# Moving layer 0's transposed state in rows of 128 bytes, so that the stationary tiles of the mix are contiguous

## Chip, cores, metric

One core of a Trainium2 chip. The metric is the time of one execution on the device in microseconds; the median of several runs is quoted. Everything is fp32.

## The reference, cut to what matters

64 graphs of 256 nodes and 128 features go through four layers. Layer 0 is a gated graph network of five steps; each step multiplies the state h by the adjacency (the mix), then updates it by gates. Layers 1 to 3 do not touch the change.

```python
def step(h, _):                                    # h: (graph, node, feature)
    m_in = jnp.einsum('nm,bmd->bnd', in_matrix, h) # the mix; in_matrix = out_matrix = adj
    ...
    z = jax.nn.sigmoid(av @ w3_w.T + w3_b + u3)
    r = jax.nn.sigmoid(av @ w4_w.T + w4_b + u3)
    hv = jnp.tanh(av @ w5_w.T + w5_b + (r * h @ u5_w.T + u5_b))
    h = (1.0 - z) * h + z * hv
```

## The kernel before

Graphs are handled in 32 pairs. A list scheduler puts the operations of all pairs in order ahead of time, from costs written in the code, so the order on TensorE is fixed and some pairs are always in flight together. The gates work on hT (features on the partitions, 4 chunks of 128 nodes along the row). The mix needs the nodes on the partitions, so after every step but the last, hT is turned into htok: VectorE transposes blocks of 32x32 into S, and four moves, one for each group of 32 source partitions, spread S over the 128 partitions of htok. Partition 4s+x then holds node 32x+s of each chunk, and aTs is the adjacency with its rows in that order.

```python
def turn(src, dst):
    S = flat("S", 3)
    add(DVE, 690, lambda: nc.vector.transpose(S.ap.rearrange("p (x r c) -> p x c r", x=4, c=4),
                                              src.ap.rearrange("p (c x s) -> p x c s", x=4, c=4)), [src], [S], [S])
    def f():
        for k in range(4):
            nc.sync.dma_start(dst.ap[:, 32 * k:32 * k + 32].rearrange("p r c -> p (r c)"),
                              S.ap[32 * k:32 * k + 32].rearrange("s (x f) -> s x f", x=4))
    add(SP, 1720, f, [S], [dst], [dst])

def mix(src, m, also, chunk=lambda src, c: src.ap[:, c, :]):
    t = bank()
    def f():
        for b in range(2):
            for j in range(2):
                nc.tensor.matmul(t.ap[:, b * N:(b + 1) * N], chunk(src, 2 * b + j), m.ap[:, j, :],
                                 start=(j == 0), stop=(j == 1))
    ...
# in the step loop: s = 0 reads x, the four others read htok
    copy(ACT, mT, mix(h, aTs, [mT], lambda src, c: src.ap[:, :, c]) if s else mix(h, aT, [mT]))
    ...
    h = temp([P, D, 4], "htok", 4)
    turn(hT, h)
```

htok is stored [feature][chunk]: a packet of a move is 32 features x 4 chunks x 4 B = 512 contiguous bytes, but the stationary tile of a chunk is 128 words at a step of 4 words.

## Time and profile before

| | before |
|---|---|
| time, median of 3 runs | 1771.41 us (1770.87 to 1772.53) |
| TensorE busy | 1692.9 us, 96% |
| matmuls with htok as stationary tile | 1024 instructions: two for each of 4 matmuls in 128 mixes |
| weight load of an htok tile / of a tile of the same shape from x | 325 / 198 ns |
| block transpose on VectorE | 1120 ns, 128 times |
| moves into htok | 512, of 64 KB, in packets of 512 B |

TensorE is pipelined: an htok matmul lasts 404 ns in the record, and the next one starts 233 ns after it. What counts is the spacing from one start to the next. Weight loads (PEld) overlap the matmuls, and in the record each other too (325 ns long, 233 ns apart); a load is called hidden here as long as it does not lengthen the spacing. The prediction shows the lines and how they are read.

### The profile page before, as it was taken

Reading aid. Unit: us, or ns where it says so; the run is one execution under the profiler, and the core shown is the slowest. Engines: PE = TensorE matmul, PEld = TensorE weight load, DVE = VectorE, ACT = ScalarE, POOL = GpSimd, SP = SyncE. Lnnn points to the kernel's source line nnn. Section 1 sums busy time; section 2 is a strip of 40 time slices with the busy share of each in tenths; the row PEclk is TensorE's granted clock in tenths of the full one; section 3 lists DMA queues with packets and bytes.
Section 4 is the critical chain, followed back from the end, with each engine's and each line's share of the span. In section 5 each row is a group of like instructions: output and inputs, shape, how many; then the busy total and the mean of one; then the engine's idle time right before and its main releaser. Section 6 shows DMA issues by size and latency. Waiting matters only on the chain.

```text
span 1771.8 us, 22424 instructions
## 1 busy us (share of the span) xinstructions
PE 1692.9 (96%) x7408; PEld 1231.7 (70%) x7408; DVE 1315.7 (74%) x3581; ACT 785.6 (44%) x1573; POOL 459.4 (26%) x487
## 2 busy tenths in 40 slices
PE   8999999999999999999999999999999999988764
PEld 5667777777777677776767777777777776755553
DVE  6577867877786887778678878878867788776543
ACT  3445444444453544445444454554444444443221
POOL 0023222222222232213323313233221223322122
PEclk9999999999999999999999999999999999998866
DMA  4100111111111111110111111101111111000000
GB/s 121 39 19 19 43 30 31 30 31 37 30 31 31 40 27 30 31 35 21 38 33 28 27 37 31 30 25 37 30 31 32 29 28 34 19 19 18 18 1 12
DMA packets 109042, 54.35 MB, mean 31 GB/s; under 512 B 9472, under 2 KB 108544, under 8 KB 108928
## 3 DMA queue, kind: packets, MB, share of 16 engines
q1 hardware_dynamic: 108640, 52.40, 11.7%
q8 instruction: 59, 0.97, 0.2%
q10 hardware_dynamic: 288, 0.53, 0.1%
q14 instruction: 55, 0.45, 0.1%
HBM read 10.95 MB, written 8.39 MB: 11 GB/s over the span
## 4 chain that ended last, share of the span: by engine, by line
PE 88%; DVE 6%; ACT 2%; POOL 1%; issue 1%; DMA 1%; SPq 1%; POOLq 0%; DVEq 0%; ACTq 0%
PE ps L459 25%; PE ps L538 7%; PE ps L535 7%; PE ps L551 7%; PE ps L553 7%; PE ps L543 7%; PE ps L687 6%; PE ps L471 6%; PE ps L434 5%; PE ps L646 3%; PE ps L696 3%; PE ps L593 2%; PE ps L635 2%; DVE st L488 1%; DVE o L517 1%
## 5 line engine op out<-in xcount | busy, mean ns | idle before, releaser
L498 POOL TENSOR_SCALAR rs<-mv 128x4 f32<-128x4 f32 x160 | 60.8, 380 | 985.4 <-DVE mv L490 976.5
L459 PEld LDWEIGHTS ps<-aTs,htok 128*128 128x128 f32 x1024 | 254.2, 325 | 40.6 <-issue 18.8
L459 PE MATMUL ps<-aTs,htok 128*128 128x256 f32 x1024 | 265.3, 404 | 10.8 <-DMA htok<-S 10.0
L499 POOL TENSOR_TENSOR rs<-rs,neg_half 128x4 f32<-128x4 f32 x192 | 212.8, 1109 | 194.6 <-DVE rs L492 178.2
L478 ACT COPY mT<-ps 128x512 f32<-128x512 f32 x160 | 93.6, 586 | 228.0 <-PE ps L459 227.8
L557 DVE TENSOR_TENSOR hv<-hv,hT 128x512 f32<-128x512 f32 x160 | 117.5, 738 | 76.5 <-ACT hv L555 75.9
L546 ACT ACTIVATE tz<-ps,bz 128x512 f32<-128x512 f32 x160 | 109.9, 688 | 139.3 <-PE ps L543 138.7
L548 DVE SCALAR_TENSOR_TENSOR tr<-tr,hT 128x512 f32<-128x512 f32 x160 | 118.2, 740 | 68.1 <-ACT tr L541 67.5
L541 ACT ACTIVATE tr<-ps,br 128x512 f32<-128x512 f32 x160 | 109.6, 687 | 130.5 <-PE ps L538 130.0
L555 ACT ACTIVATE hv<-ps,bh 128x512 f32<-128x512 f32 x160 | 109.8, 687 | 125.5 <-PE ps L553 125.1
L538 PE MATMUL ps<-mT,w4s 128*128 128x512 f32 x320 | 164.0, 598 | 1.4 <-ACT mT L478 1.4
L553 PE MATMUL ps<-tr,u5h 128*128 128x512 f32 x320 | 163.4, 596 | 1.5 <-DVE tr L548 1.4
L551 PE MATMUL ps<-mT,w5s 128*128 128x512 f32 x320 | 164.0, 595 | 0.0
L535 PE MATMUL ps<-hT,W 128*128 128x512 f32 x320 | 162.4, 596 | 1.0 <-DVE hT L560 1.0
L543 PE MATMUL ps<-mT,dw 128*128 128x512 f32 x320 | 162.4, 594 | 0.0
L442 DVE STREAM_TRANSPOSE S<-hT 128x512 f32<-128x512 f32 x128 | 142.3, 1120 | 1.8 <-issue 0.4
L459 PE MATMUL ps<-aT,x 128*128 128x256 f32 x512 | 126.4, 391 | 0.0
L511 ACT ACTIVATE x<-y,nmr,rs 128x128 f32<-128x128 f32 x256 | 105.1, 484 | 30.6 <-DVE nmr L506 30.5
L560 DVE SCALAR_TENSOR_TENSOR hT<-hv,hT 128x512 f32<-128x512 f32 x160 | 115.8, 727 | 1.8
L558 DVE SCALAR_TENSOR_TENSOR hv<-tz,hv 128x512 f32<-128x512 f32 x160 | 115.4, 724 | 1.4
L434 PEld LDWEIGHTS ps<-ident,x 128*128 128x128 f32 x512 | 65.3, 144 | 71.8 <-issue 26.2
L459 PEld LDWEIGHTS ps<-aT,x 128*128 128x128 f32 x512 | 98.5, 199 | 21.4 <-issue 7.2
(160 smaller groups left out, 2975.1 us busy)
## 6 DMA issues: line engine op xcount, KB each, us to landing
htok<-S SPq DMA_DIRECT2D x512, 64.0 KB, 2.1
x<-x_in SPq DMA_DIRECT2D x32, 256.0 KB, 2.9
y_out<-o SPq DMA_DIRECT2D x32, 256.0 KB, 2.3
W<-mats_in SPq DMA_DIRECT2D x1, 832.0 KB, 6.2
W<-mats_in ACTq DMA_DIRECT2D x1, 512.0 KB, 4.1
rbc<-rows_in SPq DMA_DIRECT2D x1, 385.0 KB, 6.9
aT<-adjT_in SPq DMA_DIRECT2D x1, 256.0 KB, 5.2
aTs<-adjT_in SPq DMA_DIRECT2D x2, 128.0 KB, 4.8
```

The costliest lines, as they stand in the source:

```text
L434: nc.tensor.transpose(t.ap[:, c * P:(c + 1) * P], chunk(c), ident.ap)
L442: add(DVE, 690, lambda: nc.vector.transpose(S.ap.rearrange("p (x r c) -> p x c r", x=4, c=4), src.ap.rearrange("p (c x s) -> p x c s", x=4 ...
L459: nc.tensor.matmul(t.ap[:, b * N:(b + 1) * N], chunk(src, 2 * b + j), m.ap[:, j, :], start=(j == 0), stop=(j == 1))
L499: nc.gpsimd.tensor_tensor(rs.ap, rs.ap, neg_half.ap, op=ALU.pow)
L535: add(PE, 865, lambda tg=tg: nc.tensor.matmul(tg.ap, mat("u3"), hT.ap, start=True, stop=False, skip_group_check=True), [hT, W0], [tg], [tg ...
L538: add(PE, 865, lambda tg=tg, mT=mT: nc.tensor.matmul(tg.ap, w4s.ap, mT.ap, start=False, stop=False, skip_group_check=True), [mT, w4s], [tg])
L543: add(PE, 865, lambda tg=tg, mT=mT: nc.tensor.matmul(tg.ap, dw.ap, mT.ap, start=False, stop=True, skip_group_check=True), [mT, dw], [tg])
L548: add(DVE, 690, lambda tr=tr: nc.vector.scalar_tensor_tensor(tr.ap, tr.ap, 1.0, hT.ap, op0=ALU.add, op1=ALU.mult), [hT], [tr])
L551: add(PE, 865, lambda tv=tv, mT=mT: nc.tensor.matmul(tv.ap, w5s.ap, mT.ap, start=True, stop=False), [mT, w5s], [tv], [tv, hv])
L553: add(PE, 865, lambda tv=tv, tr=tr: nc.tensor.matmul(tv.ap, u5h.ap, tr.ap, start=False, stop=True), [tr, u5h], [tv])
L557: add(DVE, 690, lambda hv=hv: nc.vector.tensor_sub(hv.ap, hv.ap, hT.ap), [hT], [hv])
L560: add(DVE, 690, lambda hv=hv: nc.vector.scalar_tensor_tensor(hT.ap, hv.ap, 0.5, hT.ap, op0=ALU.mult, op1=ALU.add), [hv], [hT])
```

## The change

The intent is to make the stationary tiles contiguous. htok becomes [chunk][feature]; for that, S is written in its natural order and each move's row is cut into four of 32 features, 128 bytes.

```diff
-            add(DVE, 690, lambda: nc.vector.transpose(S.ap.rearrange("p (x r c) -> p x c r", x=4, c=4),
+            add(DVE, 690, lambda: nc.vector.transpose(S.ap.rearrange("p (x c r) -> p x c r", x=4, c=4),
 ...
-                    nc.sync.dma_start(dst.ap[:, 32 * k:32 * k + 32].rearrange("p r c -> p (r c)"),
-                                      S.ap[32 * k:32 * k + 32].rearrange("s (x f) -> s x f", x=4))
+                    nc.sync.dma_start(dst.ap[:, :, 32 * k:32 * k + 32],
+                                      S.ap[32 * k:32 * k + 32].rearrange("s (y r) -> s y r", r=32))
 ...
-        def mix(src, m, also, chunk=lambda src, c: src.ap[:, c, :]):
+        def mix(src, m, also):
 ...
-                        nc.tensor.matmul(..., chunk(src, 2 * b + j), m.ap[:, j, :],
+                        nc.tensor.matmul(..., src.ap[:, 2 * b + j, :], m.ap[:, j, :],
 ...
-            copy(ACT, mT, mix(h, aTs, [mT], lambda src, c: src.ap[:, :, c]) if s else mix(h, aT, [mT]))
+            copy(ACT, mT, mix(h, aTs if s else aT, [mT]))
 ...
-                h = temp([P, D, 4], "htok", 4)
+                h = wide("htok", 4)
```

More of the change, by code (lines that the diff above doesn't have):

```diff
@@ L458, in f @@
                     for j in range(2):
-                        nc.tensor.matmul(t.ap[:, b * N:(b + 1) * N], chunk(src, 2 * b + j), m.ap[:, j, :],
+                        nc.tensor.matmul(t.ap[:, b * N:(b + 1) * N], src.ap[:, 2 * b + j, :], m.ap[:, j, :],
                                          start=(j == 0), stop=(j == 1))
```

## The prediction

> **What bounds the kernel now.** I read the page's engine table and slices first, then the chain, then the groups by shape, then one stretch of the timeline, then the moves.
>
> The first two parts of the page (busy time by engine; tenths in 40 slices):
>
> ```profile
> PE 1692.9 (96%) x7408; PEld 1231.7 (70%) x7408; DVE 1315.7 (74%) x3581; ACT 785.6 (44%) x1573; POOL 459.4 (26%) x487
> ...
> PE   8999999999999999999999999999999999988764
> ...
> PEclk9999999999999999999999999999999999998866
> ```
>
> TensorE is full in slices 2 to 35; only the first 6 us and the last five slices (some 200 us), where few pairs of graphs are left in flight, have holes. Nothing else is near full. The chain agrees:
>
> ```profile
> PE 88%; DVE 6%; ACT 2%; POOL 1%; issue 1%; DMA 1%; SPq 1%; POOLq 0%; DVEq 0%; ACTq 0%
> PE ps L459 25%; PE ps L538 7%; PE ps L535 7%; PE ps L551 7%; PE ps L553 7%; PE ps L543 7%; PE ps L687 6%; PE ps L471 6%; PE ps L434 5%; PE ps L646 3%; PE ps L696 3%; PE ps L593 2%; PE ps L635 2%; DVE st L488 1%; DVE o L517 1%
> ```
>
> So in the middle a change counts only by what it does to the spacing of TensorE's instructions; the latency of a move or of VectorE counts only where TensorE ends up waiting. Line 459 is the mix with the adjacency. The groups by shape (out<-in, count | busy us, mean ns of one | idle before):
>
> ```profile
> L459 PE MATMUL ps<-aTs,htok 128*128 128x256 f32 x1024 | 265.3, 404 | 10.8 <-DMA htok<-S 10.0 <-ACT xT L478 0.6
> L459 PE MATMUL ps<-offT,x 128*128 128x256 f32 x256 | 63.4, 392 | 0.0
> ...
> L459 PEld LDWEIGHTS ps<-aTs,htok 128*128 128x128 f32 x1024 | 254.2, 325 | 40.6 <-issue 18.8 <-PE ps L459 2.2 <-PE ps L538 1.5
> L459 PEld LDWEIGHTS ps<-offT,x 128*128 128x128 f32 x256 | 48.3, 198 | 6.2 <-issue 0.5
> ...
> L442 DVE STREAM_TRANSPOSE S<-hT 128x512 f32<-128x512 f32 x128 | 142.3, 1120 | 1.8 <-issue 0.4
> L560 DVE SCALAR_TENSOR_TENSOR hT<-hv,hT 128x512 f32<-128x512 f32 x160 | 115.8, 727 | 1.8
> ```
>
> A weight load from htok takes 325 ns, one of the same shape from x 198 ns. What differs is the layout: htok is stored feature-major with 4 chunks innermost, so a 128-column stationary tile is read at a 16-byte step. A matmul's own 404 against 392 ns overlaps its neighbours; the pace shows in the timeline (start us, length us, xcount), where a mix from htok stands near one from x:
>
> ```profile
> 799.85 2.01 PE L459 MATMUL ps<-aTs,htok 128*128 128x256 f32 x8
> ...
> 804.28 1.89 PE L459 MATMUL ps<-offT,x 128*128 128x256 f32 x8
> ```
>
> Eight matmuls take 2.01 us against 1.89. Start to start, over all of the trace, the median is 233 ns from htok and 216 ns for every other 128x256 matmul; weight loads from htok also come every 233 ns. Those mixes are paced by their weight loads, all the others by streaming.
>
> [...]
>
> **The change part by part.** The order of work on TensorE, ScalarE and GpSimd is unchanged by the change, as comparing the two programs shows; VectorE has the same instructions in the same order with another access pattern, and the SP queue the same 512 moves with another shape.
>
> Part one, stationary tiles of 4 steps x 32 pairs = 128 mixes become contiguous. Each mix has 4 fp32 matmuls issued as 8 instructions, so 1024. They should take the 216 ns pace of the others. Adding up what each htok matmul's spacing has over 216 ns (leaving out those of 260 ns and more, which waited or ran at a lower clock) gives 15.4 us; check: 128 x 7 inner spacings x 17 ns = 15.2 us. The entry into a mix costs nothing now: spacing from the instruction before is its normal 109, 112, 216 or 429 ns, so the first load is already hidden. Nearly all of it lies in the full slices, on the path: **-15.4 us**.
>
> Part two, the transpose writes contiguously. [...] from this trace, an ordinary two-input pass over 128x512 is 727 ns. [...] VectorE is not the bound, so this is worth only what it takes off a turn's latency.
>
> Part three, the moves. Each of 4 moves per turn carries 64 KB as 512 packets of 128 B in place of 128 of 512 B. These rows are from the moves by line (issues, KB each, median us to landing) and from the view of tile htok:
>
> ```profile
> htok<-S SPq DMA_DIRECT2D x512, 64.0 KB, 2.1
> ...
> y_out<-o SPq DMA_DIRECT2D x32, 256.0 KB, 2.3
> ```
> ```profile
>   DMA htok<-S: 10.0, 5
> ```
>
> The y_out store already is 512 packets (of 512 B) in one move and lands in 2.3 us: its packets start over 1.0 us, 29 ns each, 32 per engine. So generating 512 descriptors takes at most about 1.0 us. Packet durations in the trace are 9 ns (4 B), 11 ns (48 B), 27 to 29 ns (512 B uncontended); a straight line between 48 B and 512 B gives 14 ns for 128 B (estimate). Then 32 x 14 = 450 ns per engine against 8 x 29 = 230: about **+0.2 us** to landing. SP issues one move about every 0.65 us; if the engines need 0.45 us per move there is no queue, and the four stay at 2.5 us. Transpose end to last landing is 4.07 us (median) now; net, a turn gets 4.07 + 0.2[...]. Total moved bytes are equal; packets rise from 65,536 to 262,144 for htok, which at 14 ns over 16 engines is 229 us of 1771 each, far from full.
>
> What that is worth: from last landing to the mix's first weight load, the 128 turns have a slack of 0.10 us (thirteen of them, practically waiting) to 17 us, median 2.7 us, a quarter under 0.85 us. TensorE's real waits of over 0.4 us for htok are six, four of them in the tail (0.8 to 4.1 us). [...]
>
> Sum: 1771.4 - 15.4 - 1.5 = 1754.5, rounded up to 1755.
>
> **The rivals.**
> First, descriptor-bound moves. The y_out row gives only a ceiling of 1.0 us per 512 descriptors; if that is the generator's pace, not the engines', four moves take 4 us in place of 2.5[...]. From the slack of each turn, a delay of 0.5, 1.0, 1.5 and 2.0 us costs at most 7, 21.5, 41.5 and 66 us if every shortfall counted; in fact one stall delays TensorE and lets other moves catch up, so half or less. This rival then makes 1760 to 1775. For it: issue is already 602 ns, longer than y_out's 390. Against: y_out's packets are 29 ns each, 32 x 29 = 0.93 us, which explains its 1.0 us by the engines alone.
> [...]
> Third, the pace stays at 233 ns because something other than the step (the htok tile's write by moves, say) sets it: then 1769 to 1773. Against: all five other contiguous sources hold 216 ns.
> Fourth, the faster transpose frees VectorE and the end shrinks by 5 us or more: 1748 to 1750. Against: no turn is left after 1664 us, so the last 100 us is other work.
>
> **Range and chances.** 1755 us, with 1747 to 1778 holding 8 times in 10: low if the fourth rival helps, high if the first comes. Faster by 2% needs under 1736, twice what the mixes hold: 0.03. Slower by 2% needs over 1806.8, only the second rival: 0.05. Within 2%: 0.92.
>
> **What would show it.** The htok weight load at about 198 ns and the eight matmuls of a mix at 1.89 us, spacing 216: step one. [...] The htok moves landing in 2.2 to 2.5 us with issue still about 600 ns: step three; over 2.8 us, or issue stretched towards 1 us, is the first rival. TensorE waits for htok near the 10.0 us now: the sum holds; 30 us and more, and the gain has gone there. The prediction is wrong if small packets run far over 14 ns or if the weight-load pace does not move.

The sum came to 1754.5 us (1771.4 - 15.4 - 1.5): it took a turn as shorter by a time of the transpose that was in part not from the trace. With the trace's own pass of 727 ns in place of the transpose's 1120 ns, the transpose ends 0.39 us earlier and the moves land 0.2 us later; a turn is then 0.19 us shorter, six of them give 1.1 us, and the sum is 1754.9 us (an estimate from those numbers), 1755 as before. The second rival held that small packets are slow, at a packet time that no trace showed, for 1790 to 1840 us. Of a generator of descriptors the trace shows only that the 512 packets of one y_out store start over 1.0 us. That the other mixes are paced by streaming is read from the medians of the spacing in the trace of before: 111, 216 and 429 ns after matmuls of 128, 256 and 512 columns.

## The result and the profile after

The changed kernel took 1751.16 us (median of 4 runs, 1750.51 to 1752.45), the kernel before 1771.14 us in the same rounds. The ratio is 0.9888, 95% interval 0.9871 to 0.9905. A ratio is the mean time of one kernel's fast runs over that of the other's in the same rounds, so it is not quite the ratio of the medians. The gain is 1.1%, clear of noise but within the 2% that would be called faster.

Busy time and slices of the page of the changed kernel:

```profile
PE 1671.3 (95%) x7408; PEld 1179.4 (67%) x7408; DVE 1270.3 (73%) x3581; ACT 785.1 (45%) x1573; POOL 459.7 (26%) x487
...
PE   8999999999999999999999999999999999978764
```

TensorE stays the bound and has lost 21.6 us of busy time; the slices differ from those before by one digit near the end, so nothing new bounds the middle. The groups by shape of the changed kernel, to be held against those of before:

```profile
L459 PE MATMUL ps<-aTs,htok 128*128 128x256 f32 x1024 | 245.3, 384 | 9.9 <-DMA htok<-S 9.2 <-ACT xT L478 0.6
...
L459 PEld LDWEIGHTS ps<-aTs,htok 128*128 128x128 f32 x1024 | 193.4, 192 | 68.4 <-issue 33.9 <-PE ps L459 2.6 <-PE ps L551 1.2
...
L442 DVE STREAM_TRANSPOSE S<-hT 128x512 f32<-128x512 f32 x128 | 89.8, 705 | 1.8 <-issue 0.4
```

The weight load went from 325 to 192 ns, the transpose from 1120 to 705 ns. TensorE's idle time for htok's moves is 9.2 us after 10.0. In the timeline of the changed kernel a mix from htok now takes what one from x took:

```profile
804.25 1.89 PE L459 MATMUL ps<-aTs,htok 128*128 128x256 f32 x8
```

The moves of the changed kernel, from the page (packets of the whole execution, then the move by line: count, KB each, us to landing) and from the view of tile htok (issue on the SP queue, ns min/median/max):

```profile
DMA packets 305650, 54.35 MB, mean 31 GB/s; under 512 B 271616, under 2 KB 305152, under 8 KB 305536
...
htok<-S SPq DMA_DIRECT2D x512, 64.0 KB, 2.4
```
```profile
L448 SPq DMA_DIRECT2D htok<-S x512: 609/632/1633, 24.7 to 1642.5; - x171
```

The same two places for the kernel before:

```profile
DMA packets 109042, 54.35 MB, mean 31 GB/s; under 512 B 9472, under 2 KB 108544, under 8 KB 108928
```
```profile
L448 SPq DMA_DIRECT2D htok<-S x512: 542/602/2038, 24.0 to 1664.0; - x171
```

Same bytes in almost three times the packets; each move lands 0.3 us later and takes 30 ns more to issue. From the end of a transpose to the landing of the last of its four moves the median went from 4.07 to 4.46 us.

**Where the 21.4 us between the two profiled spans are.** Both traces have the same 7408 matmuls in the same order, so the spacing after each can be subtracted, pair by pair:

| spacings | saved, us |
|---|---|
| after an htok matmul, under 260 ns in both traces (964 of 1024) | 15.5 |
| after an htok matmul, the other 60 | 3.8 |
| after all other matmuls | 2.5 |
| start of TensorE in the trace | -0.4 |

The first line is 233 ns turned into 216. Of the second, 39 are the spacing after the first matmul of a mix, such as 338 to 218 ns and 413 to 291 ns; they shrank by 4.5 us together, and the other 21 grew by 0.6 us. Most of these mixes come after short matmuls (the spacing into the mix is 109 to 112 ns) or after a wait, and some 120 ns show there that do not show elsewhere. That it is the load, not hidden at this place, is the reading; e10 below supports it. The third line is of the size of the noise: a second profile of the same changed kernel (below) differs from the first by 1.6 us of span, 2.5 us of it in just these spacings, with the opposite sign in the others, and the trace of e1 (below), with a turn of the same length as before, differs from that of before by 5.8 us in them. So it is not explained further. The medians of the runs differ by 20.0 us; the first two lines make 19.3.

### The profile page after: what moved, and what is told of

It reads as the page before. It is cut to its first block, busy times and chain, and to the rows that moved or that the text cites. A ratio compares the mean times of both kernels' runs of the same rounds, so it can differ in the third digit from the quotient of the medians.

```text
span 1750.4 us, 22424 instructions
## 1 busy us (share of the span) xinstructions
PE 1671.3 (95%) x7408; PEld 1179.4 (67%) x7408; DVE 1270.3 (73%) x3581; ACT 785.1 (45%) x1573; POOL 459.7 (26%) x487
## 4 chain that ended last, share of the span: by engine, by line
PE 89%; DVE 5%; ACT 2%; POOL 1%; issue 1%; DMA 1%; SPq 0%; POOLq 0%; DVEq 0%; ACTq 0%
PE ps L459 25%; PE ps L538 8%; PE ps L543 7%; PE ps L551 7%; PE ps L553 7%; PE ps L535 7%; PE ps L687 6%; PE ps L471 6%; PE ps L434 6%; PE ps L646 3%; PE ps L696 3%; PE ps L593 2%; PE ps L635 2%; DVE st L488 1%; DVE o L517 1%
## 5 line engine op out<-in xcount | busy, mean ns | idle before, releaser
L459 PE MATMUL ps<-aTs,htok 128*128 128x256 f32 x1024 | 245.3, 384 | 9.9 <-DMA htok<-S 9.2
L459 PEld LDWEIGHTS ps<-aTs,htok 128*128 128x128 f32 x1024 | 193.4, 192 | 68.4 <-issue 33.9
L459 PEld LDWEIGHTS ps<-aT,x 128*128 128x128 f32 x512 | 98.2, 199 | 21.4 <-issue 7.7
L488 DVE BATCH_NORM_STATS2 st<-y 128x6 f32<-128x128 f32 x512 | 110.5, 278 | 0.9
```

The source lines that it names most:

```text
L459: nc.tensor.matmul(t.ap[:, b * N:(b + 1) * N], src.ap[:, 2 * b + j, :], m.ap[:, j, :], start=(j == 0), stop=(j == 1))
L488: nc.vector.bn_stats(st.ap[:, c, :], view()[:, c, :])
```

## The experiments

**Theory 1**: the reading step of the stationary tiles is the whole gain; the shorter transpose and the longer moves cancel in the latency of a turn. **Rival A**: the shorter transpose brings the gain. **Rival B**: the contiguous tiles and the shorter transpose share it. **Rival C**: small rows cost much, and a larger gain hides it. Of the runs, those marked wrong give a wrong result (data in other places, with the same instructions and dependences as far as the edit allows); the others were compared with the reference and are correct. Each was timed in 5 rounds against the kernel before.

The column "turn" is the median, over the 128 turns of the trace, of the time from the start of the transpose to the landing of the last of its four moves.

| run | tile step, words | row, B | turn, us | time, us | of before |
|---|---|---|---|---|---|
| before | 4 | 512 | 5.19 | 1770.4 to 1771.5 | 1 |
| changed, again | 1 | 128 | 5.16 | 1751.67 | 0.9892 |
| e1 step 4 (wrong) | 4 | 128 | 5.16 | 1769.71 | 0.9992 |
| e2 transpose alone (wrong) | 4 | 512 | 4.78 | 1766.79 | 0.9980 |
| e3 moves alone (wrong) | 4 | 128 | 5.58 | 1775.85 | 1.0028 |
| e5 step 2 (wrong) | 2 | 128 | 5.16 | 1752.97 | 0.9895 |
| e10 step 3 (wrong) | 3 | 128 | 5.17 | 1754.79 | 0.9905 |
| e4 pairs | 2 | 256 | 4.97 | 1751.35 | 0.9881 |
| e6 slow transpose | 1 | 128 | 5.64 | 1759.98 | 0.9936 |
| e7 rows of 64 B (wrong) | 1 | 64 | 5.57 | 1757.67 | 0.9932 |
| e8 two queues | 1 | 128 | 4.78 | 1763.17 | 0.9959 |
| e9 pairs, two queues | 2 | 256 | 3.97 | 1759.44 | 0.9929 |
| e11 pairs, one move by GpSimd | 2 | 256 | 4.33 | 1747.04 | 0.9860 |

### e1: only the reading step put back

```diff
-  mix(h, aTs if s else aT, [mT])
+  mix(h, aTs, [mT], lambda src, c: src.ap.rearrange("p y (r z) -> p (y r) z", z=4)[:, :, c]) if s else ...
```

> The changed kernel with one edit: the stationary tiles of htok are read at a step of 4 words again (of wrong columns, so the result is wrong on purpose); transpose, moves and order stay as changed. Theory 1, that the reading step alone brings the gain: loads 325 ns, spacing 233 ns, back up by 15.5 + 3.8 us, 1769 to 1772 us. Rival A, that the shorter transpose brings it: stays near 1751 us. Rival B, that contiguous tiles and the rest share it: 1758 to 1764 us.

Measured 1769.71 us, ratio 0.9992 (0.998 to 1.0005): the gain is gone, with the short transpose and the small rows still in place. The view of tile htok of this run (ns min/median/max):

```profile
L459 PEld LDWEIGHTS ps<-aTs,htok x1024: 307/329/337, 28.2 to 1665.4; 128*128 128x128 f32 x171
```

The spacing is 233 ns again (the sum over the ordinary htok spacings differs from that of before by 0.01 us). Rivals A and B fall. Transpose and moves together are worth between -3.5 and +0.9 us by the interval: nothing that can be told from zero.

### e2 and e3: the two other parts, each alone

```diff
# e2, on the kernel before
-  nc.vector.transpose(S.ap.rearrange("p (x r c) -> p x c r", x=4, c=4), ...
+  nc.vector.transpose(S.ap.rearrange("p (x c r) -> p x c r", x=4, c=4), ...
# e3, on the kernel before
-  dst.ap[:, 32 * k:32 * k + 32].rearrange("p r c -> p (r c)"),         S...("s (x f) -> s x f", x=4)
+  dst.ap.rearrange("p (y r) c -> p y (r c)", y=4)[:, :, 32*k:32*k+32], S...("s (y r) -> s y r", r=32)
```

> The kernel before with the contiguous write of the transpose alone (data lands in wrong places, wrong on purpose); moves of 512 bytes, tiles at a step of 4 words. A turn then is about 0.41 us shorter (4.06 to 3.65 us). Theory 1: only the few waits of TensorE for htok shrink, six of them by 0.4 us, 1768 to 1771 us. Rival A: near 1752 us. Transpose at about 705 ns in both.

> The kernel before with the rows of 128 bytes alone (into other places, wrong on purpose); slow transpose, tiles at a step of 4 words. A turn then is about 0.39 us longer (4.06 to 4.45 us). Theory 1, with the slack of the turns as read in the trace of before: at most 0.4 us for each of the turns without slack, together under 5 us, 1771 to 1775 us. Rival C, that small rows cost much and the change hides it by a larger gain: over 1777 us.

Measured: e2 1766.79 us, 0.9980 (0.9967 to 0.9992), 3.6 us faster; e3 1775.85 us, 1.0028 (1.0015 to 1.004), 5.5 us slower by the medians. Both lie 1 us outside what was expected, on the side of a stronger effect. The transpose in e2 and the moves in e3:

```profile
L442 DVE STREAM_TRANSPOSE S<-hT x128: 660/705/714, 22.7 to 1654.3; 128x512 f32<-128x512 f32 x128
```
```profile
htok<-S SPq DMA_DIRECT2D x512, 64.0 KB, 2.4
```

What TensorE waited for htok's moves, from the view of tile htok of e2 and then of e3 (us, times), against 10.0 us in 5 waits before:

```profile
  DMA htok<-S: 7.4, 3
```
```profile
  DMA htok<-S: 12.4, 8
```

So neither part is without effect: each moves the turn by 0.4 us, one down and one up, and the time by 3.6 and 5.5 us. In the change they stand together, and e1 shows no sum that can be told from zero. Rival C as it was put (over 1777 us) fell, but the rows of 128 B do cost, and the contiguous write of the transpose pays for it.

### e5 and e10: steps of 2 and 3 words

```diff
-  mix(h, aTs if s else aT, [mT])
+  e5:  mix(h, aTs, [mT], lambda src, c: src.ap.rearrange("p (a y) (r z) -> p a (y r) z", a=2, z=2)[:, c // 2, :, c % 2]) if s ...
+  e10: mix(h, aTs, [mT], lambda src, c: src.ap.rearrange("p c d -> p (c d)")[:, c:c + 382:3]) if s ...
```

> The changed kernel reading the stationary tiles at a step of 2 words (wrong columns, wrong on purpose). [...] the load stays near 192 ns, spacing 216, and the time 1751 us. If every step that is not 1 costs[...], the load is between 200 and 325 ns; hidden as long as it is under what 216 ns of spacing allow, so still 1751 us, else up to 1770 us.

> The changed kernel reading the stationary tiles at a step of 3 words (wrong columns, wrong on purpose). [...] load 200 to 280 ns, hidden or nearly so at 216 ns of spacing, 1751 to 1760 us. If any two words not side by side cost the same, 325 ns and 1770 us.

Measured 1752.97 us (0.9895, 0.988 to 0.9911) and 1754.79 us (0.9905, 0.9892 to 0.9919). The load at a step of 2, then at a step of 3 (view of tile htok):

```profile
L459 PEld LDWEIGHTS ps<-aTs,htok x1024: 193/196/337, 28.9 to 1649.9; 128*128 128x128 f32 x171
```
```profile
L459 PEld LDWEIGHTS ps<-aTs,htok x1024: 250/252/337, 28.9 to 1650.3; 128*128 128x128 f32 x171
```

The median load is 190, 196, 252 and 329 ns at steps of 1, 2, 3 and 4 words: a step of 2 costs 6 ns, one of 3 another 56 ns, one of 4 another 77 ns. Why it grows so is not shown. The pace is measured too: the spacing is 216 ns at steps of 1, 2 and 3, and only at 4 is it 233 ns. A load recorded at 252 ns thus fits under a spacing of 216 ns, while one of 329 ns goes with 233: the recorded length of a load is not itself the pace. At a step of 3 the trace is longer than the changed kernel's by 2.7 us, and 3.0 us of that lie in the 62 htok spacings that are not ordinary: the load shows only in those few places, the same term that the prediction left out.

### e4: rows of 256 bytes

The layout before has packets of 512 contiguous bytes and tiles at a step of 4 words; the changed one has contiguous tiles and packets of 128 B. With two chunks interleaved, rows have 256 B and the step is 2. A tile kept in four separate runs of 32 words, which would allow rows of 512 B, was not tried.

```diff
-  nc.vector.transpose(S.ap.rearrange("p (x c r) -> p x c r", x=4, c=4), src...("p (c x s) -> p x c s", x=4, c=4))
+  nc.vector.transpose(S.ap.rearrange("p (x a r z) -> p x a z r", x=4, a=2, z=2), src...("p (a z x s) -> p x a z s", ...))
-  nc.sync.dma_start(dst.ap[:, :, 32 * k:32 * k + 32], S...("s (y r) -> s y r", r=32))
+  nc.sync.dma_start(dst.ap[:, :, 32 * k:32 * k + 32, :].rearrange("p a r z -> p a (r z)"), S...("s (y f) -> s y f", f=64))
-  src.ap[:, 2 * b + j, :]                    h = wide("htok", 4)
+  src.ap[:, c // 2, :, c % 2]                h = temp([P, 2, D, 2], "htok", 4)
```

> Correct. Two chunks interleaved: rows of 256 bytes in the moves, stationary tiles at a step of 2 words, transpose writing at a step of 2 words. From the run at a step of 2, the load stays under 200 ns, spacing 216. Moves land in about 2.2 us (2.1 with 512 bytes, 2.4 with 128). [...] Theory 1 (tile reading counts, turns matter little): 1749 to 1753 us; with a short transpose 1747 to 1750 us.

The expectation left open whether the transpose takes near 1.1 us or near 705 ns.

Measured 1751.35 us, 0.9881 (0.9866 to 0.9896), beside 1751.67 us, 0.9892 (0.9879 to 0.9906), of the changed kernel, which ran again in the same rounds:

> The changed kernel unaltered, run again beside the others: 1750 to 1753 us, 0.988 to 0.990 of before.

The two cannot be told apart. The transpose of e4, writing at a step of 2 words, and its moves:

```profile
L442 DVE STREAM_TRANSPOSE S<-hT x128: 662/710/737, 24.0 to 1639.8; 128x512 f32<-128x512 f32 x128
```
```profile
htok<-S SPq DMA_DIRECT2D x512, 64.0 KB, 2.2
```

A turn is 0.19 us shorter than in the changed kernel; the transpose loses 5 ns at a step of 2 (710 ns after 705), where a step of 4 took 1114 ns before (all medians). The 1747 to 1750 us that were expected with a short transpose did not come.

### e6 and e7: a longer turn, from VectorE and from the moves

```diff
# e6: the first half of each transpose is done twice
+  [nc.vector.transpose(S...[:, :n], src...[:, :n]) for n in (2, 4)]
# e7: rows of 16 words
+  nc.sync.dma_start(dst.ap.rearrange("p c d -> p (c d)").rearrange("p (w v) -> p w v", w=8)[:, :, 16*k:16*k+16],
+                    S.ap[32*k:32*k+32].rearrange("s (y r) -> s y r", r=16))
```

> Correct. The changed kernel with the first half of each transpose done twice, so that the turn on VectorE takes about 1.1 us again (0.7 + 0.4). Theory 1: the turn gets 0.4 us longer, which cost or gave 4 to 5.5 us in the two single-part runs, so 1754 to 1758 us. Rival A (the shorter transpose is what brings the gain): near 1770 us.

> The changed kernel with moves in rows of 64 bytes (into other places, wrong on purpose): 1024 rows per move, 64 per engine. If a row takes 11 to 12 ns, 64 rows take 0.74 us per engine, more than the 0.66 us between issues, so moves begin to queue: landing 2.8 to 3.2 us, the issue near 0.75 us, a turn 0.7 to 1.0 us longer than with 128 bytes and 1755 to 1768 us. If rows cost by their bytes, nothing changes: 1751 us.

Measured: e6 1759.98 us (0.9936), 8.3 us over the changed kernel in the same rounds, for a turn 0.48 us longer; e7 1757.67 us (0.9932), 6.0 us over it, for a turn 0.41 us longer. e6 costs more than the 1754 to 1758 us that were expected, but is 11 us under before: Rival A is out once more. Its extra pass over half of the tile also lies on VectorE's queue ahead of other work, which may be why it costs more than e7; that was not taken apart. In e7 the engines did not back up as far as expected: the view of tile htok and the moves by line give

```profile
L448 SPq DMA_DIRECT2D htok<-S x512: 609/671/1892, 23.8 to 1650.6; - x171
```
```profile
htok<-S SPq DMA_DIRECT2D x512, 64.0 KB, 2.7
```

The packets of the traces took a median of 11, 13, 18 and 27 ns at 64, 128, 256 and 512 B. A straight line from 64 to 512 B gives, as an estimate, about 9 ns for any row and 3.6 ns for every 100 B ((27 - 11) ns over 448 B).

### e8, e9 and e11: a shorter turn, from sharing out the issues

The four issues take 2.65 of the turn's 5.16 us, so they are the part to cut.

```diff
# e8, on the changed kernel; e9, on e4
-  nc.sync.dma_start(...)
+  (nc.sync if k < 2 else nc.scalar).dma_start(...)
# e11, on e4
+  (nc.sync if k else nc.gpsimd).dma_start(...)
```

> Correct. The changed kernel with two of each turn's four moves issued from ScalarE's queue, two from SP: the issues overlap, so the four go out in about 1.3 us in place of 2.64 and a turn is 1.2 to 1.3 us shorter. If TensorE's waits for htok shrink as in the single-part runs (3.6 us per 0.41 us, less with each step since few turns are without slack), 1743 to 1748 us. Rival D: ScalarE, 45 percent busy, pays 256 issues of some 0.6 us, 155 us, and waits in order for each transpose, so its activations come late: 1752 to 1765 us.

> Correct. Rows of 256 bytes and tiles at a step of 2 words together with the two queues: another 0.2 us off a turn, so 1 to 2 us under the run with two queues alone, whichever way that goes.

> Correct. Rows of 256 bytes, tiles at a step of 2 words, and one of each turn's four moves issued from GpSimd's queue, three from SP. GpSimd is 26 percent busy. If its move lands before the three from SP do (some 4 us after the transpose), a turn is 0.6 us shorter and the time 1746 to 1750 us. If GpSimd, in order, is held up by waiting for the transpose, as ScalarE was with two moves, its powers for the layer norms come late and TensorE waits on those: 1753 to 1762 us.

e8 and e9 lost: 1763.17 us (0.9959, 0.9947 to 0.9972) and 1759.44 us (0.9929, 0.9916 to 0.9943), 11.5 us over the changed kernel and 8.1 us over e4 (which ran in other rounds), in spite of the shorter turn. What e8 shows of its moves, and of ScalarE's waits by shape:

```profile
htok<-S SPq DMA_DIRECT2D x256, 64.0 KB, 3.1
htok<-S ACTq DMA_DIRECT2D x256, 64.0 KB, 3.1
```
```profile
L555 ACT ACTIVATE hv<-ps,bh 128x512 f32<-128x512 f32 x160 | 109.7, 687 | 120.6 <-PE ps L553 105.4 <-DMA htok<-S 9.0 <-DVE mv L490 2.0
```

With two queues the moves of 128-byte rows land in 3.1 us, not 2.4, so the turn was only 0.4 us shorter, not the 1.2 to 1.3 expected; with 256-byte rows (e9) they land in 2.3 us, the turn is 1.0 us shorter than in e4, and e9 is 3.7 us under e8, not 1 to 2. ScalarE issues for 182 us in all, and activations that do not use htok now show waits for its moves (9.0 us in the line above, none for this activation in the changed kernel). The trace of e8 is 11.9 us longer than the changed kernel's; of its spacings, 11.2 us are lost after matmuls that have nothing to do with htok. This is what Rival D forecast, and e11, which leaves ScalarE alone, does not lose; which of ScalarE's operations is hit hardest was not isolated.

e11 gave 1747.04 us, 0.9860 (0.9844 to 0.9877), the fastest of all and correct. It was not run in the same rounds as the changed kernel; the ranges of the runs do not touch (1746.23 to 1748.3 against 1751.2 to 1752.77), and its interval just misses that of this second measurement (0.9879 to 0.9906) but meets that of the first (0.9871 to 0.9905). Against e4, from which it differs by the one issue alone, ranges and intervals overlap (e4: 1747.0 to 1752.52), so what that issue gains is not shown. GpSimd's part in it, by shape, and its moves:

```profile
L448 POOL DMA_DIRECT2D htok<-S x128 | 97.8, 764 | 362.3 <-DVE S L442 156.8 <-DVE st L488 33.9 <-PE ps L434 21.4
```
```profile
htok<-S SPq DMA_DIRECT2D x384, 64.0 KB, 2.3
htok<-S POOLq DMA_DIRECT2D x128, 64.0 KB, 2.6
```

GpSimd was idle for 362 us before these issues. Its move lands 3.16 us after the transpose (median), before the third of SP's at 3.63 us, so the turn is 0.64 us shorter than in e4.

## Why the prediction was right, and where its terms were off

- **Bound and pace (right).** The spacing went from 233 to 216 ns and gave 15.5 us against 15.4. e1 shows the step alone as the cause: with it put back, the gain is gone.
- **"The entry into a mix costs nothing now" (failed).** The spacing into a mix was indeed normal, but where a mix follows short matmuls or a wait, the cost shows in the next spacing, after the mix's first matmul (338 or 413 ns). The working had left out all spacings of 260 ns and more as waits or lower clock (13 of them, after 1609 us, are 426 or 427 ns long, where the granted clock from 1550 us on is 0.81), and these with them. The 60 spacings gave 3.8 us more. This is most of the difference between 1755 and 1751; e10, where a load of 252 ns costs just there, shows the term again.
- **The transpose (right).** 705 ns, 22 ns under the pass of 727 ns that it took from the trace.
- **The moves (right in kind, too small).** 13 ns a packet against the estimated 14, but the turn's moves got 0.39 us longer, not 0.2. 0.16 us of it is the issue of all four (2.48 to 2.65 us), which was taken as unchanged; the rest, 0.22 us, is the last landing, as estimated. Four packets of 128 B take 52 ns for the bytes that one of 512 B moves in 27 ns, so the small ones do cost more per byte here.
- **The term of -1.5 us for a shorter turn (mis-sized).** The turn changed by 0.03 us (5.19 to 5.16), as e2 and e3 take apart: -0.41 and +0.39. Waits for htok shrank by 0.8 us. So the reason given for the term fell; what transpose and moves are worth together lies by e1 between -3.5 and +0.9 us, which holds both 0 and -1.5. Where the sum is helped by this term, that is luck.
- **The slack count (too low).** It held 7 us for a delay of 0.5 us to be the most, and half or less to be real. Delays of 0.39, 0.41 and 0.48 us cost 5.5, 6.0 and 8.3 us in e3, e7 and e6. Redone for these delays (on the trace of before for e3, of the changed kernel for the others), the count gives 4.6, 5.6 and 7.2 us in full. It takes as room the 0.10 us between landing and load that even the turns without slack have; without that room it gives 6.9, 8.1 and 10.0 us. The measured costs lie between the two, so it is the halving that failed: the costs were paid about in full. Why is open; TensorE's idle time for htok itself grew by only 2.4 us (10.0 to 12.4), 4.9 us (9.2 to 14.1) and 4.4 us (9.2 to 13.6).
- **Rivals.** Descriptor-bound moves did not come: issue went from 602 to 632 ns and landing to 2.4 us. The slow packets of the second did not come (13 ns for 128 B, 27 ns for 512 B). The pace did move. The last 220 us of the trace of before hold 3.1 us of the gain, some of it the pace, so the end did not give the 5 us of the fourth.
- **Open:** the 2.5 us in spacings that do not concern htok.

## What to carry to other kernels

On a full TensorE (96% busy), compare start-to-start spacings of equal matmuls: 17 ns in one group of 1024 was 15.5 of 21.4 us here. A longer weight load in the profile pointed at the group, but only the spacing told the cost: a load of 252 ns left it unchanged. When a layout is chosen, look at all who touch it (writer, move, reader): here the contiguous tile made the reader faster (spacing 233 to 216 ns), the writer faster (1120 to 705 ns) and the move slower (landing 2.1 to 2.4 us), and the last two cancelled. A latency that looks hidden by a median slack of 2.7 us can still cost 14 to 17 times its own length when it is paid in each of 128 turns (e3, e7, e6).
